# Layer-normalised tokens transposed by VectorE and two transfers instead of TensorE, first loads kept in rank, and a new planned order

## The chip, the cores and the metric

The kernel runs on one core of a Trainium2 chip. The metric is device time in microseconds (us), lower is better. One core has TensorE (PE, matrix products), VectorE (DVE), ScalarE (ACT), GpSimd (POOL) and SyncE (SP, which here only issues transfers), and 16 DMA engines that move data between DRAM and the on-chip memory.

## What is computed

One post-norm transformer block in float32: batch 2, 512 tokens, width 512; 32 query heads and 8 key and value heads of 128; a feed-forward of 1376 with integer weights.

```python
q, k, v = x @ Wq.T, x @ Wk.T, x @ Wv.T          # per head; q and k get an RMS norm
attn = softmax(q @ k.T / sqrt(128) + slope * (j - i), causal)
x = layernorm(x + (attn @ v) @ Wo.T)
h = silu((x @ gate.T) * gs) * ((x @ up.T) * us)
x = layernorm(x + (h @ down.T) * ds)
```

## The kernel before

**Tiles.** Tokens lie in blocks of 128, four a batch, in pairs (i, i+1). For each of the 8 key heads (groups of 4 query heads) and each pair the kernel projects q, k, v (`project`, or `project_plain` for the first pair), norms the heads (`heads`), computes scores and softmax a unit (one block of queries) at a time (`scores`), multiplies by the values (`attend`), and adds the output projection into `acc` (`project_out`, and `project_pair` for the last two groups). After the last group of a batch `norm1` normalises `acc` in place and makes `x1T`, the tokens with the 512 features on the partitions, which the feed-forward multiplies (`ffn_up`, then `ffn_down`). The last groups run batch 0 first, then batch 1, so the feed-forward of batch 0 stands beside the attention of batch 1; its first four weight columns are done for batch 0 alone.

**Products.** The large products are done by seven half-size products instead of eight (`seven`, L747 in the profile, and `inner`, L1632). These need sums of blocks of both factors (`sums_a`, `sums_b`, L688, on DVE or POOL). Results come in PSUM banks a, b, c, which a copy or an add on ACT or DVE must empty before the next product of that bank.

**Names in the profile.** pp: first projection (L867). pa_q, pb_q, pc_q: later projections. sc: scores (L1263). pr: probabilities. pa<-prT: product with the values (L1408). px, pz: its remainders (L1440). pa_o, pb_o, pc_o: output projection. ptx: the transposes of `norm1` (L1781), copied to x1T (L848 on ACT, L850 on DVE). pa_h, pb_h, pc_h: gate and up products, with x1T and its sums tx. pa_d and so on: down. w and wo: weights of a group, 4 x 384 KB and 1 MB. Probabilities are turned without PE: DVE transposes blocks of 32 x 32 into st (L968), one transfer writes st to DRAM (far<-st), one or two read it back in another order (prT<-far). The heads of q and k go the same way (c, far_q, qT).

**What sets the order.** A planner written in the kernel (`Work.order`) places every operation on an engine and in time, by a cost for each (`pe`, `act`, `dve`, `pool_tt`), by priorities, and by when buffers come free; each engine then executes its list in that order. Where an operation may go to several engines the planner picks. A transfer costs its megabytes over 0.3 plus fixed parts, and transfers go one after the other; nearly all are issued by SP, in list order, each after its own waits. Before planning, the priorities are moved by random draws for the seeds in `SHIFTS` (`shift`). `WHO` names the engines that may scale the heads by their norm (in `heads`: L1065 on ACT, L1072 on DVE or POOL).

The first group's weights are loaded in four chunks of 128 input features by SP (`load_qkv`), the tokens' chunks by ACT's queue (`load_x`); their priorities are -9 to -8.97 and the draws move them like all others. At its start PE does 14 transposes on a constant (`warm`, L554).

Of the kernel before, what the change touches and what calls it, by code (L numbers as in the profile page):

```python
# [18 lines left out]
P = 128  # L19
# [11 lines left out]
Q = 32  # L31
# [33 lines left out]
def dve(n):  # L65
    return 0.15 + 0.00106 * n
# [6 lines left out]
def pool_ts(n):  # L73
# [3 lines left out]
LAG = {"PE": 0.22, "DVE": 0.1, "ACT": 0.12, "POOL": 0.2, "SP": 0.1, "ACTQ": 0.1, "NONE": 0.0}  # L77
TABLE = 1.28
SHIFTS = (
    42000001, 42000003, 42000019, 42000038, 42000046, 42000048, 42000080, 42000095, 42000168,  # L80
    42000176, 42000217, 42000257, 42000262, 42000308, 42000360, 42000448, 42000460, 42000471,
    42000478, 42000488, 42000493, 42000503, 42000508, 42000510, 42000517, 42000520, 42000530,
    42000532, 42000548, 42000582, 42000707, 42000844, 42000865, 42000884, 42000922, 42000957,
    42000970, 42000975, 42001005, 42001037, 42001049, 42001090, 42001148, 42001238, 42001283,
    42001404, 42001444, 42001471, 42001476, 42001778, 42002042, 42002048, 42002090, 42002122,
    42002149, 42002330, 42002340, 42002665, 42002784, 42002821, 42003002, 42003036, 42003133,
    42003139, 42003188, 42003348, 42003694, 42003791, 42004290, 42004466, 42005040, 42005857,
    42006497, 42006735, 42006892, 42007003, 42007117, 42007158, 42007651, 42008481, 42008514,
    42009150, 42011723, 42012356, 42012546, 42013135, 42013648, 42014108, 42014321, 42014614,
    42014976, 42015318, 42015996, 42016788, 42016932, 42017026, 42017104, 42017164, 42020579,  # L90
    42020641, 42021783, 42021971, 42022454, 42022740, 42023193, 42023363, 42024350, 42024865,
    42025415, 42026349,
)
NORMED = {"DVE": dve(5 * HD) + 0.2, "POOL": pool_tt(5 * HD), "ACT": 5 * act(HD, True)}
WHO = ("DVE", "POOL", "ACT")
ALONE = lambda p, r: False


# [65 lines left out]
class Work:  # L164
# [166 lines left out]
    def shift(self, seed):  # L331

        rnd = random.Random(seed)
        at, reach, by = rnd.uniform(-9, 100), rnd.choice((1, 3, 8, 30)), rnd.choice((0.1, 0.3, 1.0))
        moved = {}
        for o in self.ops:
            if abs(o["first"] - at) < reach:
                key = o["first"], tuple(sorted(o["costs"]))
                if key not in moved:
                    moved[key] = rnd.gauss(0, by)  # L340
                o["prio"] += moved[key]

    def emit(self):
        for seed in SHIFTS:
# [9 lines left out]
def post_ln_block(  # L354
# [116 lines left out]
    def load(mb, prio, fn, writes, reads=(), queue="SP", after=()):  # L471
        engine = {"SP": nc.sync, "ACTQ": nc.scalar}
        queues = (queue,) if isinstance(queue, str) else queue
        W.add({k: mb / 0.3 for k in queues}, prio, lambda e: fn(engine[e]), reads, writes, after)

    w_qkv, w_o, t_q, t_o, t_i = {}, {}, {}, {}, {}

# [1007 lines left out]
    def y_half(t, n):  # L1485

        b, i = divmod(t, NTB)
        return acc[b][:, 2 - i // 2 + 2 * n, i % 2, :]
# [8 lines left out]
    def y_keys(t, ns=(0, 1)):  # L1497
        b, i = divmod(t, NTB)
        return [key for n in ns for key in cell_keys(b, 2 - i // 2 + 2 * n, i % 2)]
# [222 lines left out]
    def layernorm(t, prio, dst, dst_keys, name, pieces=1, after=()):  # L1722
# [43 lines left out]
            )  # L1766
        return ve_op

    x1T, tx = {}, {}

    def norm1(t, prio):
        b, i = divmod(t, NTB)
        layernorm(t, prio, lambda: y_row(t), y_keys(t), f"a{t}")
        pt = Buf(r_po, f"ptx_{t}")
        if i == 0:
            x1T[b] = Buf(r_xT, f"x1T_{b}")
        xb = x1T[b]

        def transposes(e):
            for kc in range(NK):  # L1780
                nc.tensor.transpose(  # L1781
                    pt[:, ts(kc, P)], y_half(t, kc // 2)[:, ts(kc % 2, P)], ident.tile
                )

        W.add(
            {"PE": NK * TR}, prio, transposes, y_keys(t) + [A(ident)], [A(pt)]
        )
        copy_op(
            S,
            prio,  # L1790
            lambda: xb[:, :, ts(i, P)],
            lambda: pt.tile.rearrange("p (kc c) -> p kc c", kc=NK),
            [A(pt)],
            [(xb, i)],
        )
        if i == NTB - 1:
            tb = Buf(r_sx, f"tx_{b}")
            tx[b] = tb
            sums_b(
                2 * NTH,  # L1800
                prio,
                lambda j: tb[:, j - 1],
                lambda r, n: xb[:, 2 * r : 2 * r + 2, n * NTH : (n + 1) * NTH],
                lambda j: (tb, j),
                lambda r, n: [(xb, 2 * n), (xb, 2 * n + 1)],
            )
# [123 lines left out]
    def ffn_up(fc, b, weights, prio):  # L1930

        fw = min(P, DFF - fc * P)
        key = f"{fc}_{b}"
        wf, sw = weights
        gu, sg = Buf(r_gu, f"gu_{key}"), Buf(r_sg, f"sg_{key}")
        if b not in hT:
            hT[b] = Buf((r_h0, r_h1)[b], f"hT_{b}")
        h, xb, tb = hT[b], x1T[b], tx[b]
        homes = ((r_f, r_f, r_f), (r_sc, r_sc, r_po))[turn[0] % 2]
        turn[0] += 1  # L1940

        def copy(n, bank):
            copy_op(
                NTH,
                prio,
                lambda: gu[:fw, n, :],
                lambda: bank[:fw, :NTH],
                [A(bank)],
                [(gu, n)],
                ("ACT",),  # L1950
            )

        def add(n, bank):
            tensor(
                NTH,
                prio,
                lambda: gu[:fw, n, :],
                lambda: bank[:fw, :NTH],
                lambda: gu[:fw, n, :],
                ALU.add,  # L1960
                [A(bank), (gu, n)],
                [(gu, n)],
                ("DVE",),
            )

        def done(which, bank):
            if which == 1:
                copy(0, bank)
            elif which == 2:
                add(0, bank)  # L1970
            elif which == 6:
                copy(1, bank)
            elif which == 7:
                copy(3, bank)
            elif which == 5:
                add(3, bank)
            elif which == 4:
                copy(2, bank)
            else:
                add(1, bank)  # L1980
                finish()

        def finish():
            gcol, ucol = lambda: gs_sb[:fw, fc : fc + 1], lambda: us_sb[:fw, fc : fc + 1]
            gate = lambda: gu[:fw, 0:2, :].rearrange("p n c -> p (n c)")
            W.add(
                {"ACT": act(S, True)},
                prio,
                lambda e: nc.scalar.activation(sg[:fw, :], gate(), AF.Sigmoid, scale=gcol()),
                [(gu, 0), (gu, 1), A(gs_sb)],  # L1990
                [A(sg)],
                table="sigmoid",
            )
            W.add(
                {"DVE": 0.75},
                prio,
                lambda e: nc.vector.scalar_tensor_tensor(
                    sg[:fw, :], gate(), gcol(), sg[:fw, :], ALU.mult, ALU.mult
                ),
                [(gu, 0), (gu, 1), A(gs_sb), A(sg)],  # L2000
                [A(sg)],
                port=True,
            )
            W.add(
                {"DVE": 0.75},
                prio,
                lambda e: nc.vector.scalar_tensor_tensor(
                    h[:fw, fc, :],
                    gu[:fw, 2:4, :].rearrange("p n c -> p (n c)"),
                    ucol(),  # L2010
                    sg[:fw, :],
                    ALU.mult,
                    ALU.mult,
                ),
                [(gu, 2), (gu, 3), A(us_sb), A(sg)],
                [(h, (fc, 0)), (h, (fc, 1))],
                port=True,
            )
            finished.append(W.ops[-1])

        def a_ap(f, ch):
            if isinstance(f, tuple):
                return wf[:, f[0], 2 * f[1] + ch, :fw]
            return sw[:, f - 1, ch, :fw]

        def a_keys(f):
            return [(wf, f[0])] if isinstance(f, tuple) else [(sw, f)]

        def b_ap(f, ch):
            if isinstance(f, tuple):  # L2030
                return xb[:, 2 * f[0] + ch, f[1] * NTH : (f[1] + 1) * NTH]
            return tb[:, f - 1, ch, :]

        def b_keys(f):
            return [(xb, 2 * f[1]), (xb, 2 * f[1] + 1)] if isinstance(f, tuple) else [(tb, f)]

        seven(prio, Factor(a_ap, a_keys), Factor(b_ap, b_keys), fw, NTH, 2, f"h{key}", done, homes)
# [206 lines left out]
```

## Time and profile before

| | before |
|---|---|
| median of 3 runs | 952.7 us (951.93 to 955.5) |
| profiled execution | 954.71 us, span of its instructions 952.9 us |
| granted TensorE clock, mean | 0.997 |
| PE busy in 0 to 40 us | 35.93 us |
| PE busy in 40 to 640 us | all but 0.04 us |
| PE busy in 640 to 720 us | 77.28 of 80 us, clock 1.00 and 0.96 |
| PE busy in 920 us to the end | 27.06 us |
| ptx transposes (L1781) | 32, first at 702.5, last at 761.2 us |
| transfers over the whole span | 157.46 MB, 165 GB/s |

A matrix product in float32 leaves two records in the trace, a transpose by PE one. Lengths of neighbouring PE records overlap[...]; what a product costs PE is the distance to the next start. In lines of the timeline a number in square brackets is idle time before the group, and what ended it. "SPq" lines are the issues of transfers, not their length. The chain of work that ended last follows the last instruction back to what released it.

### The profile page before, as it was taken

The page shows a single profiled execution, that of the slowest core. Times are in us where ns is not written, and L with a number is a line of the kernel's source. Part 1 is how long each engine was busy: PE and PEld are TensorE (multiplying, and loading weights), DVE is VectorE, ACT ScalarE, POOL GpSimd, SP SyncE. Part 2 cuts the span into 40 slices and gives each one's busy share as a digit, 9 for nine tenths or more (in the row PEclk, how much of TensorE's full clock was granted, in tenths as well). Part 3 has the DMA queues.
Part 4 walks back from the last instruction along what each step waited for, and adds up shares of the span by engine and source line. Part 5 has one row for each costly group of instructions (what it writes and reads, how often), then busy time and mean ns, then how long its engine had stood idle before and what let it go on. Part 6 is the DMA issues. An engine that isn't in the chain of part 4 may idle for free.

```text
span 952.9 us, 14098 instructions
## 1 busy us (share of the span) xinstructions
PE 940.2 (99%) x4254; PEld 682.6 (72%) x4254; DVE 713.3 (75%) x1767; ACT 485.2 (51%) x1347; POOL 549.3 (58%) x608
## 2 busy tenths in 40 slices
PE   8999999999999999999999999999999999999997
PEld 5655776766767675767677766676677888888886
DVE  7777877778877878887878888787776766675464
ACT  3676665656565656465746566565652433433100
POOL 5774775657494837775768686866564412232040
PEclk9999999999999999999999999999999999999999
DMA  9269758555583847657678786569852323310011
GB/s 324 67 199 258 232 157 241 170 184 174 176 234 107 267 132 222 206 186 198 172 239 225 235 214 190 174 184 263 217 176 81 86 81 89 85 52 23 1 45 44
DMA packets 196876, 157.46 MB, mean 165 GB/s; under 512 B 28384, under 2 KB 179680, under 8 KB 195520
## 3 DMA queue, kind: packets, MB, share of 16 engines
q1 hardware_dynamic: 195936, 155.90, 54.8%
q8 instruction: 34, 0.56, 0.2%
q10 hardware_dynamic: 864, 0.66, 0.2%
q14 instruction: 42, 0.34, 0.1%
HBM read 97.60 MB, written 58.46 MB: 164 GB/s over the span
## 4 chain that ended last, share of the span: by engine, by line
PE 96%; DMA 2%; SPq 1%; DVE 0%; issue 0%; POOLq 0%; DVEq 0%
PE pa_q L747 17%; PE sc L1263 13%; PE pa L1408 12%; PE pb_q L747 8%; PE pa_h L747 8%; PE pa_o L1632 8%; PE pb_h L747 4%; PE pc_q L747 4%; PE pb_o L1632 4%; PE pa_d L747 4%; PE pa_o L747 3%; PE pc_o L1632 2%; PE pc_h L747 2%; PE pb_d L747 2%; PE px L1440 2%; DMA prT<-far 2%
## 5 line engine op out<-in xcount | busy, mean ns | idle before, releaser
L1288 ACT ACTIVATE pr<-pr,nmax 128x48 f32<-128x48 f32 (+15 forms) x256 | 133.4, 522 | 91.2 <-DVE nmax L1272 90.1
L1263 PE MATMUL sc<-kT,qT 128*128 128x512 f32 (+15 forms) x512 | 154.1, 409 | 0.0
L1272 DVE CUSTOM_DVE_ANT_0 pr<-sc,bias 128x48 f32<-128x48 f32 (+15 forms) x256 | 109.7, 442 | 34.3 <-PE sc L1263 31.5
L1408 PE MATMUL pa<-prT,v 128*128 128x512 f32 (+1 forms) x306 | 129.6, 512 | 2.7 <-DMA prT<-far 2.7
L1263 PEld LDWEIGHTS sc<-kT,qT 128*128 128x128 f32 x512 | 88.2, 191 | 48.2 <-issue 21.9
L1320 ACT ACTIVATE pr<-pr,rden 128x64 f32<-128x64 f32 (+12 forms) x221 | 95.4, 495 | 23.1 <-DVE rden L1303 22.8
L688 DVE TENSOR_TENSOR acc<-acc,pa_o 128x512 f32<-128x512 f32 (+2 forms) x128 | 72.7, 568 | 44.9 <-PE pa_o L1632 28.2
L968 DVE STREAM_TRANSPOSE st<-pr 128x512 f32<-128x512 f32 (+1 forms) x153 | 92.1, 634 | 1.6 <-ACT pr L1320 0.6
L747 PE MATMUL pa_q<-tq,sx 128*128 128x384 f32 x248 | 90.3, 487 | 0.0
L1408 PEld LDWEIGHTS pa<-prT,v 128*128 128x128 f32 x306 | 54.0, 191 | 24.3 <-issue 6.4
L674 POOL TENSOR_TENSOR inv<-ms,nhalf 128x10 f32<-128x10 f32 (+1 forms) x33 | 64.9, 1966 | 7.8 <-DVE ms L1039 5.4
L848 ACT COPY gu<-pa_h 128x256 f32<-128x256 f32 (+1 forms) x88 | 31.8, 370 | 73.3 <-PE pa_h L747 62.7
L1002 ACT ACTIVATE sq<-c 128x640 f32<-128x640 f32 x64 | 45.7, 730 | 38.3 <-DVE c L1188 32.9
L747 PEld LDWEIGHTS pa_q<-tq,sx 128*128 128x128 f32 x248 | 45.5, 190 | 26.9 <-issue 5.5
L848 ACT COPY c<-pa_q 128x384 f32<-128x384 f32 x73 | 34.5, 473 | 54.2 <-PE pa_q L747 47.4
L1065 ACT ACTIVATE sq<-c,inv 128x128 f32<-128x128 f32 x165 | 51.9, 397 | 15.0 <-POOL inv L674 15.0
L1188 DVE STREAM_TRANSPOSE c<-sq 128x320 f32<-128x320 f32 x124 | 55.8, 485 | 0.0
L1025 DVE TENSOR_REDUCE ms<-sq 128x5 f32<-128x640 f32 x64 | 51.4, 810 | 1.2 <-ACT sq L1002 1.2
L1632 PEld LDWEIGHTS pa_o<-ti,si 128*128 128x128 f32 x336 | 43.1, 192 | 7.2 <-issue 3.6
L688 POOL TENSOR_TENSOR so<-aT,aT 128x512 f32<-128x512 f32 x23 | 29.3, 1274 | 32.8 <-PE pa_o L1632 31.7
L1322 POOL TENSOR_SCALAR pr<-pr,rden 128x64 f32<-128x64 f32 (+7 forms) x67 | 31.1, 473 | 29.4 <-DVE rden L1303 28.3
L1288 ACT ACTIVATION_READ_ACCUMULATOR pr<-pr,nmax 128x1 f32 x256 | 48.0, 188 | 0.0
(245 smaller groups left out, 2216.9 us busy)
## 6 DMA issues: line engine op xcount, KB each, us to landing
far<-st SPq DMA_DIRECT2D x122, 256.0 KB, 3.1
prT<-far SPq DMA_DIRECT2D x244, 128.0 KB, 3.2
far_q<-c SPq DMA_DIRECT2D x31, 640.0 KB, 3.9
qT<-far_q SPq DMA_DIRECT2D x62, 320.0 KB, 3.8
w<-in_wqkv_dram SPq DMA_DIRECT2D x39, 384.0 KB, 4.6
wo<-in_wot_dram SPq DMA_DIRECT2D x10, 1024.0 KB, 5.8
far<-st SPq DMA_DIRECT2D x31, 128.0 KB, 2.7
prT<-far SPq DMA_DIRECT2D x62, 64.0 KB, 3.0
```

The lines of the kernel that those rows point to most:

```text
L674: lambda e: nc.gpsimd.tensor_tensor(dst(), src(), nhalf[:, :n], ALU.pow),
L688: lambda e: vec[e].tensor_tensor(dst(), a(), b(), alu),
L747: nc.tensor.matmul(bank[:rows, :width], lhsT=a(fa, c), rhs=b(fb, c), start=(fresh and c == 0), stop=(c == depth - 1), skip_group_check=True,)
L848: nc.scalar.copy(dst(), src())
L968: {"DVE": dve(n)}, prio, lambda e: nc.vector.transpose(dst(), src()), reads, [A(st)]
L1188: lambda e, r=r, m=m: nc.vector.transpose(cb[:, m] .rearrange("p n w -> p (n w)")[:, :half] .rearrange("p (m r h d) -> p r h m d", m=2, r= ...
L1263: lambda e, a=a, w=w, sc=sc: nc.tensor.matmul(sc[:, :w], lhsT=qT[:, r, a, : G * Q], rhs=kT[:, :w], start=True, stop=True),
L1272: lambda e, a=a, w=w, sc=sc: nc.vector.tensor_tensor_reduce(out=pr[:, a, :w], in0=sc[:, :w], in1=bias[:, S - w :], scale=-(SHRINK**-g), sc ...
L1288: lambda e, a=a, w=w: nc.scalar.activation(pr[:, a, :w], pr[:, a, :w], AF.Exp, bias=nmax[:, a : a + 1], scale=-1.0, accum_out=den[:, a : a ...
L1320: nc.scalar.activation(dst, src, AF.Copy, scale=rden[:, a : a + 1])
L1408: lambda e, j=j, prT=prT, n=n: nc.tensor.matmul(by_head(po.tile)[:, :, P - n // G :], lhsT=v[:, j, :], rhs=late(prT, j, n), start=(j == 0) ...
L1632: nc.tensor.matmul(bank[:, ts(c, P)], lhsT=a(fa, c), rhs=b(fb, c), start=fresh and c == 0, stop=True, skip_group_check=True,)
```

## The change

1. `norm1`: the four PE transposes of a block and the copy to x1T go. Instead DVE transposes each half of the block in squares of 32 x 32 into `st_x` (which takes a buffer of prT's ring), a transfer writes it to DRAM (`far_x`), and a second reads it back into x1T. The features then lie on the partitions in another order, and a token block in x1T as runs of 32 columns; the rows of the gate and up weights are reordered to match on the host, and sums and products read x1T through `by_tokens`.
2. The random draws leave operations whose first priority is -8 or less where they are, among them the first loads of w and x.
3. `WHO` loses DVE: heads are scaled by POOL or ACT.
4. Transfers are planned at 0.26 MB per us.
5. `SHIFTS` is another list (74 seeds for 110), so the whole order is drawn anew.

```diff
 SHIFTS = (
-    42000001, 42000003, 42000019, 42000038, 42000046, 42000048, 42000080, 42000095, 42000168,
...
+    112000003, 112000009, 112000014, 112000024, 112000026, 112000038, 112000041, 112000056,
...
-WHO = ("DVE", "POOL", "ACT")
+WHO = ("POOL", "ACT")
...
-                o["prio"] += moved[key]
+
+                if o["first"] > -8:
+                    o["prio"] += moved[key]
...
-        W.add({k: mb / 0.3 for k in queues}, prio, lambda e: fn(engine[e]), reads, writes, after)
+        W.add({k: mb / 0.26 for k in queues}, prio, lambda e: fn(engine[e]), reads, writes, after)
...
+    def by_tokens(xb, n):
+
+        a = NTH // Q
+        return xb.tile.rearrange("p n c -> p (n c)").rearrange("p (a k q) -> p a k q", k=NK, q=Q)[
+            :, n * a : (n + 1) * a
+        ]
...
-        def transposes(e):
-            for kc in range(NK):
-                nc.tensor.transpose(
-                    pt[:, ts(kc, P)], y_half(t, kc // 2)[:, ts(kc % 2, P)], ident.tile
-                )
-
-        W.add(
-            {"PE": NK * TR}, prio, transposes, y_keys(t) + [A(ident)], [A(pt)]
-        )
-        copy_op(
-            S,
-            prio,
-            lambda: xb[:, :, ts(i, P)],
...
+        st = Buf(r_prT, f"st_x{t}")
+        for n in range(2):
+            W.add(
+                {"DVE": dve(WO)},
+                prio + 0.1,
+                lambda e, n=n: nc.vector.transpose(
+                    st.tile.rearrange("p (m k q) -> p k m q", m=NQ, k=NK)[:, 2 * n : 2 * n + 2],
+                    y_half(t, n).rearrange("p (k m d) -> p k m d", k=2, m=NQ),
+                ),
+                y_keys(t, (n,)),
+                [(st, n)],
+            )
+        far = Buf(r_far, f"far_x{t}")
+        load(
+            0.26,
+            prio + 0.1,
+            lambda q: q.dma_start(far.tile.rearrange("(p c) -> p c", p=P), st.tile),
+            [A(far)],
+            [(st, 0), (st, 1)],
+        )
+        load(
+            0.26,
+            prio + 0.1,
+            lambda q: q.dma_start(
+                xb.tile.rearrange("p n c -> p (n c)")[:, ts(i, S)].rearrange(
+                    "p (a c) -> p a c", a=NQ
+                ),
+                far.tile.rearrange("(a d c) -> d a c", a=NQ, d=P),
+            ),
             [(xb, i)],
+            [A(far)],
         )
...
-                return xb[:, 2 * f[0] + ch, f[1] * NTH : (f[1] + 1) * NTH]
+                return by_tokens(xb, f[1])[:, :, 2 * f[0] + ch, :]
...
+    def by_partition(w):
+        return w.reshape(NK, NQ, Q, DFF).swapaxes(1, 2).reshape(DM, DFF)
...
-        "gwt": a["L0_ffn_gate_w"].T,
+        "gwt": by_partition(a["L0_ffn_gate_w"].T),
...
-        "uwt": a["L0_ffn_up_w"].T,
+        "uwt": by_partition(a["L0_ffn_up_w"].T),
```

## The prediction

> **What bounds the kernel now.** I read the engine totals first, then TensorE's (PE's) waits, then its timeline where it loses time.
>
> ```profile
> PE 940.2 (99%) x4254; PEld 682.6 (72%) x4254; DVE 713.3 (75%) x1767; ACT 485.2 (51%) x1347; POOL 549.3 (58%) x608
> PE 96%; DMA 2%; SPq 1%; DVE 0%; issue 0%; POOLq 0%; DVEq 0%
> PE pa L1408 <- DMA prT<-far: 2.7, 2, 2.1
> PE pp L867 <- DMA w<-in_wqkv_dram: 1.8, 1, 1.8
> PE pp L867 <- DMA xT<-in_xt_dram: 0.4, 1, 0.4
> ```
>
> The first line is the busy time, the second the chain that ended last, the others PE's waits (total, times, longest). PE is busy 99% and is 96% of the chain, so only two things count: the length of PE's own work, and its few holes. Work on the other engines matters only where it makes a hole.
>
> PE's own work is measured by slots, from one start to the next:
>
> ```profile
> 702.46 0.60 PE L1781 MATMUL ptx<-ident,acc 128*128 128x128 f32 x4
> 702.89 1.03 PE L747 MATMUL pa_o<-to,aT 128*128 128x256 f32 x4
> 703.76 0.59 PE L1408 MATMUL pa<-prT,v 128*128 128x256 f32 x2
> 704.19 1.03 PE L747 MATMUL pb_o<-wo,so 128*128 128x256 f32 x4
> ```
>
> Columns: start, length, line, tile, records. Four transposes hold PE 702.89 - 702.46 = 0.43 us; four 256-column records 0.87 (the printed lengths overlap). A record costs 0.844 ns a column; a product has two records, a transpose one. Summed over PE's list this is 935.5 us before. The span is 952.9. The rest, about 17, is the start (5.0 to the first real product, 1.8 and some 0.5 lost in the first projection), about 6 after the last product, and holes in between.
>
> ```profile
> 5.04 3.06 PE L867 MATMUL pp<-w,xT 128*128 128x384 f32 x8 [0.44 <-DMA xT<-in_xt_dram]
> 9.87 7.98 PE L867 MATMUL pp<-w,xT 128*128 128x384 f32 x24 [1.77 <-DMA w<-in_wqkv_dram]
> 17.68 1.45 PE L747 MATMUL pa_q<-w,xT 128*128 128x384 f32 x4
> ...
> 677.58 0.35 SPq L541 DMA_DIRECT2D wo<-in_wot_dram  x1
> 678.01 3.53 SPq L1385 DMA_DIRECT2D prT<-far  x4
> ...
> 688.09 2.05 PE L1408 MATMUL pa<-prT,v 128*128 128x512 f32 x2 [2.11 <-DMA prT<-far]
> ```
>
> ```profile
> 686.00:688.00 2.00, 0.00 (x0) 0.00 (x0) 1.03 (x4) 0.00 (x0) 0.00 (x0) 1.00 1.20 213
> 688.00:689.00 1.00, 0.92 (x1) 0.50 (x2) 0.00 (x0) 0.00 (x0) 0.00 (x0) 0.50 1.11 348
> 690.00:691.00 1.00, 1.00 (x5) 0.91 (x4) 0.28 (x2) 0.11 (x1) 0.00 (x0) 0.50 0.33 116
> 691.00:692.00 1.00, 1.00 (x4) 0.80 (x4) 0.05 (x1) 0.37 (x2) 0.00 (x0) 0.79 0.06 21
> ```
>
> The windows show PE, PEld, DVE, ACT, POOL busy, then granted clock, DMA share, GB/s. At 677.58 a 1 MB load of wo goes into the queue just ahead of the prT reads; the reads take some 7 us to land and PE stands. After this 2.1 us hole the clock is 0.50 until about 691.3.
>
> **Part 1, transposes off PE.** 8 token blocks x 4 transposes leave PE: 8 x 0.43 = 3.46 us, and all other products are the same ones (slot sum 932.0). These transposes lie where PE has no other idle time, so all 3.46 come off the end. Gone too are 8 copies x1T<-ptx (ACT 6 x 0.59, DVE 2 x 0.69).
>
> Added: 16 DVE transposes of 256 columns. The nearest row is L968's 128x256 form, 0.43 us: 6.9 us of DVE. Added: 8 writes far_x and 8 reads x1T of 256 KB on SP's queue, by far<-st (3.1 us to land) and prT<-far (3.2; qT<-far_q of 320 KB 3.8). SP pays about 0.5 us to issue each.
>
> Their latency is covered for batch 1: its last out-projection product ends at slot 730.1 of the new order, and the first product that reads its late tokens starts at 746.6. The path between is add 0.42, statistics 0.86 + 0.21 + 0.15, pow 0.7, scaling 0.54, transposes 0.86, write 3.1, read 3.2 = 10.0 us against 16.5. Batch 0 has 28 (675.4 to 703.4). Without that cover each batch would pay about 6.
>
> Here a rule speaks against the change. The Trainium skill, page "DMA: Bandwidth & Descriptors", section "Rules for kernel authors", says not to transpose by a plain DMA with a rearranged pattern, which it puts at 19 times slower. Taken literally, 19 x 3.2 = 61 us, 45 over batch 1's cover: far slower. But the element transposition is done by VectorE; the DMA only moves rows of 128 floats, and 306 prT reads of this kind landed in about 3 us. I take the row.
>
> x1T is now read by PE as 8 runs of 32 columns, not 256 in a row. No row shows runs of 32; the nearest, L1408's 256-column form, reads 4 runs of 64 and holds the same 0.43 us for two records (703.76 to 704.19). I take nothing; the other end is a rival. VectorE's sums over x1T keep their element counts; cost between 0 and some tenths on DVE, nothing on PE.
>
> **Part 2, first loads keep their rank.** Before, the loads of w in the first projection came as chunks 0, 3, 2, then 1 behind qw and kw, while PE consumed 0, 1, 2, 3; of x's loads the second half of chunk 0 was second and its first half fourth. So PE waited for the last load. The first projection is 32 x 0.324 = 10.4 us of slots and took 17.68 - 5.04 = 12.6: 2.3 lost, and 0.44 before it. In the new order the loads follow PE's use. By the rates of this stretch (about 0.37 MB per us from 4 to 7 us, 1.16 MB up to chunk 1, 2.1 MB in all) chunk 1 is there at about 6 us, chunk 3 at about 8, each before PE asks. I take 2.3 saved, bounds 1.0 and 2.7.
>
> Something comes back: row 0's products now end first but both rows end later in the projection, GpSimd has a 1.8 us weight sum before the reciprocal root, and the transposes of unit 1's probabilities stand directly before their product (copy about 0.55 + lags against 0.43 of cover). I charge 0.4, between 0 and 1.2. Net: -1.9.
>
> **Part 3, transfers planned at 0.26 MB per us, own shifts.** These change only order, and new waits can appear anywhere. Before, the holes at 648 and 688 cost 0.85 + 2.33, and the slow clock 1.2 more: 4.4 us. Behind the same wo load the new order has 17.8 us of PE slots from a unit's last score to its first value product, where it had 16.1; with 2.1 missing then, and the read pushed behind four small vn loads, this one is close but I expect it to hold.
>
> A new knot stands at slots 668 to 690. There DVE carries in one row the adds of batch 0's last pairs, six statistics, four scalings and eight new transposes, while SP holds wo, two x1T reads and then prT. Summing DVE's list from slot 668 with its own durations (add 0.36 issue to issue, transpose 0.37, score reduction 0.3 to 0.65), the score reduction of 432 columns ends at about 681.2; PE wants its bank at 680.3. The add that frees the next bank ends at about 686, PE wants it at 684.6. That makes 1.7 us in two holes. SP adds its own wait: each x1T read is issued only when its far_x has landed, and the prT reads of units 1 and 0 of batch 1 are queued behind. The prT read behind 1 MB + 0.5 MB may miss by 1 more. So 2.8 in place of 4.4: -1.6; bounds -4.4 and +1.5.
>
> The second rule decides the price of such a hole. The same skill, page "TensorE: Matmul & The Clock Gate", Part 1, throttles after an idle window of about 3.4 us. By that, holes of 1 to 2 us cost only themselves. The trace had 0.50 after 2.1 us, but 1.00 after 1.8 us at 10 us. I use the row: a hole of 2 us or more costs 1.2 on top, hence the +1.5.
>
> **Part 4, heads times norm off VectorE.** DVE had 7 of them (L1072, 1.10 mean); now six more on GpSimd (1.26 each) and one more on ScalarE (5 x 0.39). DVE loses 7.7, gains 6.9 by the transposes, loses 1.4 by the copies: even. GpSimd gets 7.6 more at 58% load. PE waited for none of these except 0.5 at 20.9; nothing.
>
> **Sum.** -3.5 - 1.9 - 1.6 = -7.0 us. The profiled execution took 954.71 (span 952.9), so it would be 947.7; the median of the runs before is 952.7, 2.0 lower, so I put the median after at 945.7.
>
> **Rivals.**
> (a) The knot costs as much as the old holes, or more: a hole over 2 us with the half clock, and the start gives 1.0 to 1.9. For it: DVE's list above, and 1.5 MB ahead of prT. Against: the two holes come out under 2 us each. Time: -3.5 - 1.5 + 0 to 1.5, about 948.5.
> (b) No new hole at all and the whole start gain: -3.5 - 2.7 - 4.0 = 942.5. For: from 40 to 640 us the old order had none.
> (c) Slower: PE reads x1T in runs of 32 more slowly. Place: 352 records of pa_h, pb_h, pc_h with x1T, 352 x 0.216 = 76 us. Price: a quarter more is +19, so 952.7 - 7.0 + 19 = 964.7. It decides from about 15% more on (11.8 us). Against it: runs of 64 read at full rate.
> (d) The loads do not land in order of rank, so the start gains nothing: 945.7 + 1.9 = 947.6.
>
> **Chances.** Forecast 0.50; (a) 0.22; (b) 0.10; (c) 0.07; (d) 0.11. A measurement of this kernel can tell about 0.5% (4.8 us) from no change, so faster means under 947.9, slower over 957.5. Of the forecast nearly all is faster, (b) all, (d) half, (a) a third: 0.70. Slower is (c) and a worse knot: 0.08. The rest, 0.22, is within. The range leaves out (c) and the ends of (a) and (b): 942.3 to 950.5.
>
> **What would show it.** No ptx rows, PE about 3.5 us less busy; the pp products in one row from about 5 us, the next projection at 15 to 16 us; no hole over 1 us from 40 to 640 us; holes of 1 to 2 us between 675 and 695, released by DVE (acc, nmax) or prT, with clock 1.00; pa_h on x1T at 0.43 a pair; 16 transposes at 0.43. It is wrong if the 256-column records of the feed-forward stretch out, if DMA x1T shows among PE's waits, or if the clock falls to 0.50 again.

## The result and the profile after

| | before | after |
|---|---|---|
| median, 7 runs each | 952.47 us (951.93 to 955.5) | 957.12 us (955.82 to 958.29) |
| ratio, 95% interval | | 1.0045 [1.0035, 1.0055] |
| profiled execution, span | 954.71, 952.9 us | 957.12, 955.3 us |
| TensorE's products, summed by slots, px and pz once a pair | 921.7 us | 918.2 us |
| transfers | 157.46 MB | 161.65 MB |

The change makes the kernel slower by 0.45%, some 4.6 us, where 7.0 us less were forecast. The totals of the page after, and its chain:

```profile
PE 938.4 (98%) x4222; PEld 677.3 (71%) x4222; DVE 722.3 (76%) x1785; ACT 475.5 (50%) x1329; POOL 554.0 (58%) x620
PE 91%; DMA 3%; DVE 2%; POOL 2%; issue 1%; ACT 0%; SPq 0%; ACTq 0%; POOLq 0%; DVEq 0%
```

The 32 transposes are gone (4254 records became 4222) and TensorE's work is 3.46 us shorter, as forecast. (The prediction's 935.5 and 932.0 count the 64 pairs of px and pz one after the other, but the two of a pair start together, as in these lines of before's timeline. Counted once, at 0.216 us a pair, the products come to 13.8 us less: 921.7 of before's 952.9 us, which leaves 31 us outside them and not 17. The difference between the kernels stays.)

```profile
678.10 0.38 PE L1440 MATMUL px<-prT,v 64*128 64x256 f32 x1
678.10 0.38 PE L1440 MATMUL pz<-prT,vs 64*128 64x256 f32 x1
```

TensorE's share of the chain that ended last fell from 96% to 91%: other engines and transfers now stand in it more. TensorE's waits after:

```profile
PE pa L1407 <- ACT pr L1319: 2.2, 1, 2.2
PE pb_q L746 <- DVE xT L687: 1.5, 1, 1.5
PE pa_h L746 <- ACT gu L847: 1.4, 3, 0.5
...
PE pa L1407 <- ACT prT L847: 0.9, 1, 0.9
PE pp L866 <- DMA xT<-in_xt_dram: 0.9, 1, 0.9
PE pa_h L746 <- DVE sw L687: 0.8, 1, 0.8
```

Apart from the first transposes, before waited over a microsecond in two places, both times for transfers. After waits for DVE and ACT where before did not. The first line is another matter. It is the hole at 696, and the profile names ACT for it, but this product multiplies prT, and the pr that is named ended at 698.68, long after the reads of this prT had been issued:

```profile
687.85 3.28 SPq L976 DMA_DIRECT2D far<-st  x4
691.31 1.55 SPq L1211 DMA_DIRECT2D qT<-far_q  x2
692.97 5.27 SPq L1384 DMA_DIRECT2D prT<-far  x8
698.34 1.02 SPq L1801 DMA_DIRECT2D far_x<-st_x  x2
...
698.80 1.10 PE L1407 MATMUL pa<-prT,v 128*128 128x512 f32 x2 [2.20 <-ACT pr L1319]
```

The first two prT reads, issued at 692.97 and 693.65, landed at 698.04 and 698.66, 5.0 us after their issue, and the product started at 698.80. So this too was a wait for a transfer, behind four writes of probabilities and the heads' transfers. Part 1's first transfer, far_x, was issued only at 698.34 and has no part in it.

Where the time is lost is seen best from starts: a record's distance to the next start, less its slot (0.844 ns a column), is time that TensorE lost. Summed by stretch of each profiled execution, in us ("again" is the first experiment; the 1.3 ahead of the first record and the 6.0 behind the last are left out):

| stretch, us | before | before, again | after |
|---|---|---|---|
| 0 to 40 | 5.5 | 5.4 | 5.2 |
| 40 to 120 | 1.3 | 1.6 | 3.9 |
| 120 to 520 | 8.1 | 8.0 | 8.3 |
| 520 to 640 | 2.9 | 3.6 | 3.1 |
| 640 to 720 | 5.9 | 2.6 | 4.9 |
| 720 to the end | 0.2 | 0.2 | 4.4 |
| sum | 23.9 | 21.4 | 29.8 |

Against the second execution of before, which stands close to the median of its kernel, after loses 8.4 us more in holes and has 3.5 less work: 4.9 us, and the spans differ by just that (950.4 and 955.3). The start, from after's timeline:

```profile
4.38 3.09 PE L866 MATMUL pp<-w,xT 128*128 128x384 f32 x8
8.33 8.01 PE L866 MATMUL pp<-w,xT 128*128 128x384 f32 x24 [0.86 <-DMA xT<-in_xt_dram]
16.17 1.45 PE L746 MATMUL pa_q<-w,xT 128*128 128x384 f32 x4
...
20.40 1.53 PE L746 MATMUL pb_q<-w,xT 128*128 128x384 f32 x4 [1.48 <-DVE xT L687]
```

The next projection starts at 16.17 instead of 17.68, so 1.5 us are won; four microseconds later pb_q waits 1.48 for DVE, where it waited 0.51 before, and starts at 20.40 instead of 20.93. And the feed-forward's start, again after's timeline, with ACT's copies:

```profile
760.72 0.37 ACT L847 COPY gu<-pa_h 128x256 f32<-128x256 f32 x1 [1.28 <-PE pa_h L746]
...
761.14 1.13 PE L746 MATMUL pa_h<-tx,sw 128*128 128x256 f32 x4 [0.46 <-ACT gu L847]
762.31 0.37 ACT L847 COPY gu<-pa_h 128x256 f32<-128x256 f32 x1 [1.22 <-PE pa_h L746]
...
762.74 1.13 PE L746 MATMUL pa_h<-tx,wf 128*128 128x256 f32 x4 [0.46 <-ACT gu L847]
```

Four of the seven products of a block add up in one bank, and each sum must be copied out before the next is added. With nothing in between, a product starts 1.60 us after the one before it (761.14 to 762.74), not 0.86: the bank's turn costs 0.74 us beyond the slot. In before, the products of two blocks of weight columns (both of batch 0, by the kernel's list) take turns at this place, each in other banks, and every start is 0.86 after the last:

```profile
754.38 1.03 PE L747 MATMUL pa_h<-tx,sw 128*128 128x256 f32 x4
755.24 1.03 PE L747 MATMUL pa_h<-x1T,wf 128*128 128x256 f32 x4
756.11 1.03 PE L747 MATMUL pa_h<-tx,sw 128*128 128x256 f32 x4
756.97 1.03 PE L747 MATMUL pc_h<-x1T,wf 128*128 128x256 f32 x4
```

### The profile page after: what moved, and what is told of

Same layout as the page of the kernel before. It is cut to its first block, busy times and chain, and to the rows that moved or that the text cites. A ratio compares the mean times of both kernels' runs of the same rounds, so it can differ in the third digit from the quotient of the medians.

```text
span 955.3 us, 14135 instructions
## 1 busy us (share of the span) xinstructions
PE 938.4 (98%) x4222; PEld 677.3 (71%) x4222; DVE 722.3 (76%) x1785; ACT 475.5 (50%) x1329; POOL 554.0 (58%) x620
## 2 busy tenths in 40 slices
DMA packets 202252, 161.65 MB, mean 169 GB/s; under 512 B 28640, under 2 KB 184032, under 8 KB 200896
## 4 chain that ended last, share of the span: by engine, by line
PE 91%; DMA 3%; DVE 2%; POOL 2%; issue 1%; ACT 0%; SPq 0%; ACTq 0%; POOLq 0%; DVEq 0%
PE pa_q L746 16%; PE sc L1262 12%; PE pa L1407 11%; PE pb_q L746 8%; PE pa_o L1631 8%; PE pa_h L746 8%; PE pb_h L746 4%; PE pb_o L1631 4%; PE pc_q L746 4%; PE pa_d L746 4%; PE pa_o L746 2%; PE pc_o L1631 2%; PE pc_h L746 2%; PE pb_d L746 2%; PE px L1439 2%; PE pb_o L746 1%
## 5 line engine op out<-in xcount | busy, mean ns | idle before, releaser
L1287 ACT ACTIVATE pr<-pr,nmax 128x384 f32<-128x384 f32 (+15 forms) x256 | 133.5, 522 | 86.9 <-DVE nmax L1271 85.9
L1262 PE MATMUL sc<-kT,qT 128*128 128x304 f32 (+15 forms) x512 | 153.2, 407 | 0.2 <-DVE nmax L1271 0.2
L1271 DVE CUSTOM_DVE_ANT_0 pr<-sc,bias 128x384 f32<-128x384 f32 (+15 forms) x256 | 109.5, 441 | 28.6 <-PE sc L1262 25.3
L1407 PE MATMUL pa<-prT,v 128*128 128x256 f32 (+1 forms) x306 | 128.1, 509 | 2.5 <-ACT pr L1319 2.2
L1319 ACT ACTIVATE pr<-pr,rden 128x64 f32<-128x64 f32 (+10 forms) x214 | 92.0, 494 | 19.5 <-DVE rden L1302 19.5
L1321 POOL TENSOR_SCALAR pr<-pr,rden 128x256 f32<-128x256 f32 (+12 forms) x74 | 34.7, 479 | 52.6 <-DVE rden L1302 52.0
L849 POOL CAST wf<-wi 128x512 f32<-128x512 int32 (+1 forms) x15 | 9.0, 603 | 72.5 <-PE pa_h L746 35.0
```

The lines of the kernel that those rows point to most:

```text
L1262: lambda e, a=a, w=w, sc=sc: nc.tensor.matmul(sc[:, :w], lhsT=qT[:, r, a, : G * Q], rhs=kT[:, :w], start=True, stop=True),
L1271: lambda e, a=a, w=w, sc=sc: nc.vector.tensor_tensor_reduce(out=pr[:, a, :w], in0=sc[:, :w], in1=bias[:, S - w :], scale=-(SHRINK**-g), sc ...
L1287: lambda e, a=a, w=w: nc.scalar.activation(pr[:, a, :w], pr[:, a, :w], AF.Exp, bias=nmax[:, a : a + 1], scale=-1.0, accum_out=den[:, a : a ...
L1319: nc.scalar.activation(dst, src, AF.Copy, scale=rden[:, a : a + 1])
L1407: lambda e, j=j, prT=prT, n=n: nc.tensor.matmul(by_head(po.tile)[:, :, P - n // G :], lhsT=v[:, j, :], rhs=late(prT, j, n), start=(j == 0) ...
```

## The experiments

Theory A: part 1 is worth its 3.46 us, and the loss lies in the newly drawn order. Theory B: part 1 comes back as waits, since the tokens now arrive later than the order can hide. To tell them apart, parts had to be changed without a new draw. So the runs below (except the first, and the one that is drawn anew on purpose) execute a written list instead of the planner's choice; the list starts as the planner's own for before or after, and only what is named in it changes:

```diff
     def emit(self):
-        for seed in SHIFTS:
-            self.shift(seed)
-        for o in self.order():
+        for o in self.replay(PLACED):
```

PLACED holds each operation and its engine, in order; `replay` gives out buffers as `order` did. Line numbers in these runs' profiles are higher by about 170 (L917 is L747 of before). "Placed anew" means that in a stretch the priorities were drawn some thousand times, and the list with the planner's earliest end was kept.

**Before, a second time.** No edit.

> The kernel before, unchanged, profiled a second time. The first profiled execution (954.71 us) lay 2.2 us above the median of its kernel's runs and had a hole of 2.3 us at 686 followed by a half clock until 691, about 3.3 us together. If that hole belongs to the order, it is there again and the execution takes about 954.7. If it is a chance of that one execution (a transfer that just missed), the hole is under 1 us here, the clock stays at 1.00, and the execution takes about 952.5; then there was less for part 3 to save than the 4.4 us of the prediction.

Measured: 952.21 us. The wait at 686, from its list of TensorE's waits:

```profile
PE pa L1408 <- DMA prT<-far: 0.8, 1, 0.8
```

A hole of 1.0 us, clock 1.00. The kernel's runs show the same split: of 51 later runs of before, the 5 with a mean clock of 0.996 or 0.997 have a median of 955.0, the other 46 of 952.9. The execution from which the prediction was worked out (clock 0.997) was one of the long ones.

**Part 1 alone, in the order of before.**

```diff
 before.py with norm1, by_tokens and by_partition of the change
 PLACED: before's up to 680 us of the plan; placed anew behind it
```

> Part 1 alone. The order of before is written out and kept on every engine up to about 690 us; behind it the operations are placed anew, with the best of some thousand draws for this case. First loads, rates and GpSimd's share stay as before. If part 1 is worth its 3.46 us of transposes, as the prediction has it, the time is 952.5 - 3.5 = 949.0. If the longer way of the tokens through DVE and two transfers comes back as waits of TensorE (four products of one pair that share a PSUM bank stand one behind the other at the start of the feed-forward, 0.63 us each, because batch 1 is not there yet), it is 952 to 955, with holes of 0.6 us and one of 1.5 between 735 and 765.

Measured: 954.33, ratio 1.0018 [1.0011, 1.0025]. From its timeline:

```profile
758.01 1.10 PE L917 MATMUL pa_h<-tx,sw 128*128 128x256 f32 x4 [0.66 <-ACT gu L1018]
759.58 1.13 PE L917 MATMUL pa_h<-tx,sw 128*128 128x256 f32 x4 [0.46 <-ACT gu L1018]
761.17 1.13 PE L917 MATMUL pa_h<-tx,wf 128*128 128x256 f32 x4 [0.46 <-ACT gu L1018]
```

The same waits as after has, in another order: behind 720 us TensorE loses 5.1 us here where before loses 0.2. Part 1 is not worth 3.46 us here; it costs 1.6.

**Part 2 alone, in the order of before.**

```diff
 SP:   w chunks 0a 0b 3 2 (qw kw) 1   ->  0a 0b 1 2 3 (qw kw)
 ACTQ: x chunks 1 0b 3 0a 2           ->  0b 0a 1 2 3
```

> Part 2 alone. The order of before is written out and kept; only the first loads of w and x change places among themselves, into the order of their rank (x: the half that TensorE uses first goes first). The prediction's step says 1.9 to 2.3 us less: 950.4. The rival: the next projection starts 1.5 us earlier (16.2 instead of 17.7), but its third product waits for the sums of x, which stand on DVE and GpSimd behind the bias and the mean squares, and starts no earlier than before (20.9): no change, 952.5 within 0.5.

Measured: 952.76, ratio 0.9998 [0.9989, 1.0006]. TensorE's timeline, and DVE's:

```profile
16.08 1.45 PE L917 MATMUL pa_q<-w,xT 128*128 128x384 f32 x4
17.37 1.45 PE L917 MATMUL pc_q<-w,xT 128*128 128x384 f32 x4
20.32 1.53 PE L917 MATMUL pb_q<-w,xT 128*128 128x384 f32 x4 [1.50 <-DVE ms L1209]
```

```profile
17.41 0.81 DVE L1195 TENSOR_REDUCE ms<-sq 128x5 f32<-128x640 f32 x1
18.25 0.42 DVE L1209 TENSOR_SCALAR ms<-ms 128x5 f32<-128x5 f32 x1
18.57 0.54 DVE L1020 COPY c<-pa_q 128x384 f32<-128x384 f32 x1
19.04 0.80 DVE L1195 TENSOR_REDUCE ms<-sq 128x5 f32<-128x640 f32 x1
19.77 0.41 DVE L858 TENSOR_TENSOR xT<-xT 128x256 f32<-128x256 f32 x1
```

pa_q starts 1.6 us earlier, and pb_q only 0.6 (20.32 against 20.93). It needs the sum over x (19.77), which stands on DVE behind the mean squares without a gap. (The bracket names ms, which ended last before the start; the product reads xT.) Of the 0.6 left nothing is seen at the end.

**After without part 1, order kept.**

```diff
 after.py with norm1 of before (PE transposes, copies); each transpose placed as early as its tokens allow
```

> The changed kernel with its order written out and kept, and part 1 alone undone: the transposes are back on TensorE, each as early as its tokens allow, the eight pairs of transfers and sixteen DVE transposes are gone. If part 1 saves its 3.46 us, this is 957.1 + 3.5 = 960.6. If it gives them back as waits in this order (684 to 702 us, where its transfers stand among those of the probabilities, and 759 to 770), this is 957 to 957.6, with the holes at 696 and at 760 to 768 smaller or gone.

Measured: 958.41, ratio 1.0057 [1.0044, 1.0070], against after's 1.0045. Part 1 gives 1.3 us of its 3.46 in after's order (the two intervals overlap a little, so this is no more than likely). The rest of the change, without part 1, costs 5.7 us (958.41 against 952.75). So each theory holds in part: A for the order, which costs most, and B for part 1, of which much comes back as waits. The same sums over starts say where the order loses: against the second execution of before this run loses 2.7 us more from 40 to 80 us, 1.3 more from 640 to 720 and 3.0 more behind 720, and 0.8 less elsewhere. Of the waits for a bank at the feed-forward's start two of after's three are still there (at 762 and 770), and so is a hole of 1.7 us at 697.

**After, its first 58 us placed anew.**

```diff
 PLACED: after's, what starts before 58 us placed anew
```

> The changed kernel with all its parts; its order is written out, and only what stands in the first 58 us is placed anew (the best of some thousand draws), the rest is kept on every engine. The changed kernel has holes of 1.7 us at 18, and 1.1, 0.5 and 0.7 between 43 and 53. If the loss of 4.7 us against before lies in the new draw there, it is about 4 us less than the changed kernel: 953. If it lies in part 1's waits at 684 to 770, the start gives at most the 1 us at 18 back: 956.

Measured: 955.86, ratio 1.0036 [1.0023, 1.0049]: near the second of the two forecasts, 1.3 us less than after (the intervals overlap). TensorE lost 3.0 us less up to 80 us (5.2 became 3.1 up to 40 us, 2.7 became 1.9 behind it), but the hole at 692 was 2.7 us with the half clock behind it, where after's is 2.4 with full clock (640 to 720 us: 6.8 against 4.9). What the start wins, that stretch can take back in one execution.

**Part 1 for batch 0 only, in the order of before.**

```diff
     def norm1(t, prio):
+        (norm1_dma if t < NTB else norm1_pe)(t, prio)
 PLACED: before's up to 670 us of the plan; placed anew behind it
```

> The order of before up to about 680 us, and part 1 for batch 0 only: its 16 transposes go through DVE and transfers, batch 1's 16 stay on TensorE (the features of the accumulator lie in another order on the host's side, so that both ways give the same x1T). If part 1 fails only where its way is not covered, batch 0 (28 us of cover) gives its 1.73 us: 951.0, and no holes of 0.6 us between 740 and 770. If the transfers around 690 or the reads in runs of 32 are the cause, it is as slow as part 1 for both batches: 954.3.

Measured: 951.41, ratio 0.9987 [0.9978, 0.9996]: 1.3 us of the 1.73. From its timeline:

```profile
756.69 1.03 PE L917 MATMUL pa_h<-tx,wf 128*128 128x256 f32 x4
757.56 1.03 PE L917 MATMUL pb_h<-x1T,sw 128*128 128x256 f32 x4
758.42 1.04 PE L2013 MATMUL ptx<-ident,acc 128*128 128x128 f32 x8
```

Every start is 0.86 after the last; no product waits for a bank. So the reads in runs of 32 and the transfers of batch 0 are not what costs: what costs is batch 1's way, or the order that it leaves to the planner.

**The start placed anew in before; and the same with the identity made first.**

```diff
 PLACED: before's from 55 us on, first loads by rank, before 55 us placed anew
 second run: POOL  order, ident  ->  ident, order
```

> The kernel before with its order kept from 55 us on; the first loads go by rank, and the first 55 us are placed anew, so that the sums of x no longer stand behind DVE's mean squares. If the first projection's gain was lost only to that list of DVE, 1.5 to 2 us come off: 950.5 to 951.0, with no hole over 0.7 us before 60 us. If another wait takes its place, it stays at 952.7.

> The kernel of the run with the start placed anew in before (no change in its time, since TensorE's first transposes then waited 1.5 us longer for GpSimd's identity), with only two operations of GpSimd exchanged: the identity is made first again. If that wait took the whole gain, 1.5 us come off: 951.2, the first transposes start at 1.35, and no wait over 0.7 us stands before 60 us. If the start is not worth anything, 952.7.

Measured: 952.87, ratio 1.0004 [0.9995, 1.0014], and 954.11, ratio 1.0009 [1.0000, 1.0019]. Neither gives the 1.5 us. In the first, TensorE's first transposes wait until 2.81 us for GpSimd instead of 1.35. In the second that is mended, but a product was placed ahead of its chunk of x and waits 1.0; and the hole at 686 was 3.2 us with the half clock. Up to 640 us this run loses as much as before's second execution does (18.6 us each). No order tried here keeps what the start wins.

**Part 2 as the diff has it, planner left free.**

```diff
-                o["prio"] += moved[key]
+                if o["first"] > -8:
+                    o["prio"] += moved[key]
```

> Part 2 as the diff has it, alone, in the kernel before: three lines of it, the rank of the first loads kept, and the planner left to place everything with the old draws. Written into a kept order the same edit took 0.0 us. If an edit costs what its own work costs, this is 952.7 again, or 950.4 by the prediction's step. If the draws fit only the costs they were made for, the whole order falls apart and holes of 0.5 to 2 us appear everywhere: 20 to 30 us slower, 975 to 982.

Measured: 979.74, ratio 1.0288 [1.0266, 1.0310]. Some of its waits of TensorE:

```profile
PE pa L1410 <- DMA prT<-far: 4.5, 3, 1.7
PE ptq L1147 <- ACT sq L1067: 2.4, 1, 2.4
PE sc L1265 <- DVE nmax L1274: 2.2, 3, 1.7
```

The same edit took 0.0 us in a kept order and 27 with the order drawn anew: 12.9 us lost up to 40 us (5.1 of them in 10.2 us at a clock of 0.50), 4 at 80, 5 at 400, 7.4 at 680. The draws fit one set of inputs.

**The load of wo moved; and left out.**

```diff
 SP at 678 us
-wo
 prT prT prT prT qT prT prT
+wo
 far far far
 second run: no load; GpSimd sets the tile to zero, at 696 us
```

> The kernel before in its own order, with one transfer moved: the load of wo (1 MB) that stood ahead of the prT reads at 678 us stands behind them. The hole at 686 was 1.0, 2.0, 2.3, 2.5 and 1.7 us in five profiled executions of this order. If the wo load makes it, the hole goes below 0.5 us and the time falls by 1 to 2 us, to 951.2. If the transfers of the scores alone keep the DMA engines full there, the hole stays or moves to the next product: 952.7.

> The kernel before in its own order without the 1 MB load of wo at 678 us: GpSimd fills the tile with zeros instead, in a gap of its list at 686, so this leaves out the weights of one group for batch 1. If the stretch from 676 to 697 us is bound by its transfers, the hole at 686 (1.0 to 2.5 us) goes below 0.4, none takes its place at 692, and the time falls by 1.5 to 2: 951. If the chain of the last scores is what ends late, the hole stays: 952.7.

Measured: 952.67, ratio 0.9996 [0.9984, 1.0008], and 951.56, ratio 0.9976 [0.9967, 0.9986]. Windows of the first and of the second (PE, PEld, DVE, ACT, POOL busy, clock, DMA share, GB/s):

```profile
684.00:690.00 6.00, 6.00 (x27) 4.47 (x27) 5.01 (x20) 4.30 (x17) 2.62 (x5) 1.00 0.89 300
690.00:697.00 7.00, 5.35 (x20) 3.51 (x19) 4.08 (x14) 2.25 (x6) 3.68 (x6) 1.00 0.59 183
```

```profile
684.00:690.00 6.00, 6.00 (x28) 4.47 (x28) 4.99 (x20) 3.77 (x15) 2.11 (x5) 1.00 0.56 180
690.00:697.00 7.00, 7.00 (x26) 4.51 (x25) 5.60 (x18) 2.84 (x8) 4.76 (x8) 1.00 0.80 244
```

Moved, the load lets go of the product at 686 and holds up the one at 692 (1.65 us missing there). Left out, TensorE has no hole in either window, and 1.8 us come off. So the stretch from 676 to 697 is bound by what it has to move, whichever transfer stands first.

**Part 4 alone, in the order of before.**

```diff
 PLACED: seven scalings of heads, DVE -> POOL, places kept
```

> Part 4 alone, in the kept order of before: the seven scalings of heads by their norm that DVE did stand at the same places on GpSimd. The prediction's step says no change (952.7). The rival: the slower engine (1.26 us against 1.10, and a longer list) makes the heads late in places, up to 1.5 us at 43 and 217 us: 954.

Measured: 953.28, ratio 0.9998 [0.9990, 1.0006]: nothing, as forecast.

**What was tried to add up.**

```diff
 PLACED: the list with part 1 for batch 0; up to 600 us the list with the mended start; wo moved as above
```

> What held of the change, with its covers: part 1 for batch 0 only, the first loads by rank with the first 55 us placed anew and the constant that TensorE's first transposes need made first, and the 1 MB load of wo moved behind the prT reads; all else in the order of before. If the three gains add: 1.3 (measured for batch 0) + about 1.5 (start) + about 1 (hole at 686) below before: 949. If they do not add, because each frees time that the next wait takes, 951.

Measured: 951.79, ratio 0.9984 [0.9976, 0.9992]. That is no more than part 1 for batch 0 alone gives, within the intervals. In its profiled execution a product waited 2.1 us for xT at 6 us, and the half clock followed. Part 1 for batch 0 stays the simplest version that beats both kernels, by 0.13% [0.04, 0.22] against before.

## Why the prediction was wrong, point by point

Two steps failed. The larger is part 3: a newly drawn order was priced at -1.6 us, from the stretches of it that were followed, and measures about +5.7. The other is part 1's "Their latency is covered for batch 1": the way took 16.7 us instead of 10.0, and the products that were to cover it waited themselves.

**The base.** The sum was made against an execution of 954.71 us, 7.0 were taken off, and the 2.0 us between that execution and the median were taken off as well. But those 2.0 us were largely the long hole at 686 and the half clock behind it, which part 3 had already counted as saved. The second execution of before (952.21) shows 1.0 us there. So about 2 us were counted twice.

**Part 1: "all 3.46 come off the end".** TensorE's work fell by 3.46. TensorE's reads of x1T in runs of 32 cost nothing (rival (c) is refuted by the 0.86 us between starts in the feed-forward). The estimate of 61 us, from the factor 19 of the Trainium skill, page "DMA: Bandwidth & Descriptors", section "Rules for kernel authors" (which sets a plain DMA against the hardware's own transposing one), did not show: the eight x1T reads took 3.7 to 6.7 us to land. The row was right in kind, and too short in size. The step that failed is "Their latency is covered for batch 1", 10.0 us against 16.5. From the end of the last out-projection product (757.1) it took 5.4 us to the last transpose (3.7 forecast), 4.5 more until the last x1T read was issued (3.1) and 6.8 until the sums over x1T could start at 773.8 (3.2): 16.7 us in all.

For the late tokens themselves TensorE then stood only about 0.4 us (at 775 to 778). It lost more inside the cover, where one block's four products on one bank wait for copies. A stretch counts as cover only if it would run without waits itself. Measured: -1.3 in after's order, +1.6 in before's, -1.3 of -1.73 for batch 0 alone. Why the planner sets one block after another there, where before's list has two side by side, no run shows; that batch 1's tokens come late is the likely reason.

**Part 2: -1.9.** The loads landed in order (rival (d) is out), but the first projection gained 1.5 us and not 2.3, and the charge of 0.4 for what comes back was the mis-sized term: DVE's list takes 1.0 of the 1.5 back within 4 us, and alone the part gave 0.0.

**Part 3: -1.6, "bounds -4.4 and +1.5".** This is the term that decided. What it said of the load of wo came true: the reads behind it cost TensorE no more than 0.2 us (at 688.8). A hole did come in the stretch of the knot, 2.4 us at 696, released by prT and close to the 2.8 that was charged. But it is not the sum that gave 2.8: no bank on DVE held TensorE over 0.2 us there, and neither wo nor x1T stood ahead of the late prT read, but writes of probabilities and the heads' transfers. That the size fits is luck. The clock stayed at 1.00 in this execution, so neither the rule nor the row of the half clock mattered.

What was not priced is the sentence "new waits can appear anywhere": in a new draw they did, at 18, 43 to 54, 597, 760 to 768 and 851 us, each 0.5 to 1.7 us. Without part 1, parts 2 to 4 with their draw cost 5.7 us (958.41 against 952.75), and parts 2 and 4 alone cost 0.0 in before's order. So this term is about +5.7, not -1.6, and of the loss only 1.3 us lie in the stretch of the knot. Only the start and slots 640 to 720 were followed in the new order; the rest of it was taken to be as good as the old one. The draws of before were worth a great deal: one edit of three lines lost 27 us of it.

**Part 4: 0.** Right, -0.1 measured. (Its "even" for DVE was 2.2 us less by its own numbers; after's page has 9.0 more, 722.3 against 713.3. Neither shows in the time of the run that tried part 4 alone.)

**The sum** of the two measured terms is -1.3 + 5.7 = 4.4, against 4.6 measured. It has to close, since both terms come from one run between before and after; it says how the loss divides, and is no proof of its own.

Of what would show it, "no hole over 1 us from 40 to 640 us" failed (1.07 at 44). None of the three signs of being wrong appeared: no long records, no DMA x1T among TensorE's waits, no half clock. Nor does any rival fit: (a) and (b) forecast a gain, (c) and (d) are out, and a new order that is worse as a whole stood among neither the rivals nor the signs. Open: how much of the 5.7 belongs to the planned rate of 0.26 and how much to chance in the draws. No run separates them, since either can only act by drawing the order anew.

## What to carry to other kernels

If an order was found by search for exactly one set of inputs, any edit that makes the search's result fall elsewhere must be priced as a new order: walk its whole list for waits, not the changed stretch alone, and try the edit in the kept order first. Cover is worth its length only when the work in it runs without waits, here with two blocks taking turns; a chain that turns one bank round is not full cover. And before working out a gain from a profile, see whether that execution stands at the kernel's median, or what is saved may be a chance of that one run. A wait's named releaser is worth a second look as well: here the engine named was not what the product needed.

## What was not expected of the hardware

The half clock comes at the edge of these holes, not by one length. In the run of part 4 alone a wait of 2.1 us was followed by it (windows as above):

```profile
688.00:690.00 2.00, 1.14 (x2) 0.65 (x3) 0.00 (x0) 0.03 (x1) 0.00 (x0) 0.71 1.12 308
690.00:692.00 2.00, 2.00 (x7) 1.30 (x6) 0.28 (x2) 1.04 (x5) 0.37 (x1) 0.50 0.54 187
```

In after, a wait of 2.2 us was not:

```profile
696.00:698.00 2.00, 0.60 (x3) 0.19 (x1) 2.00 (x8) 0.44 (x2) 0.36 (x2) 1.00 1.22 203
699.00:700.00 1.00, 1.00 (x4) 0.50 (x4) 0.61 (x1) 0.34 (x3) 0.00 (x0) 1.00 1.22 222
```

Waits of 2.3, 2.5 and 3.0 us in three other runs (part 1 for batch 0, after's start, the mended start) all had it, the wait of 2.1 in part 2 alone did not. The 3.4 us of idle time that the Trainium skill, page "TensorE: Matmul & The Clock Gate", Part 1, gives for this are not what these traces show. Where it came in these executions and in the first one of before, the half clock lasted 3.4 us (688.00 to 691.42 in before), and by starts less slots TensorE lost 1.5 to 1.8 us in it, where the prediction took 1.2.
